# Cross-attention on one core: moving the last output pieces, two additions, and the closing matmuls of the last sequence

## Chip, cores and metric

The kernel runs on one core of a Trainium2 chip. Its time is device time in microseconds (us), the median of repeated runs. A profile is one further execution, taken by the hardware profiler. Engines are named as the profile names them: PE is the matmul engine (PEld its weight loads), DVE the vector engine, ACT the scalar engine, POOL the GpSimd engine, SP the engine that issues all DMAs of this kernel. L460 is line 460 of the kernel.

## What is computed

There are 32 sequences of 512 queries and 640 channels, each with its own context of 77 keys with 1024 channels, and 20 heads of 32 channels. The reference splits the keys into four sets, but the context has exactly the 77 keys of the first set, so the other three sets are empty and only this remains:

```
q = heads(x @ to_q_w)                       # (32, 20, 512, 32)
k = heads(ctx @ to_k_w); v = heads(ctx @ to_v_w)
s = einsum('bhqd,bhkd->bhqk', q, k) / sqrt(32)
p = softmax(s, axis=-1)
o = merge(einsum('bhqk,bhkd->bhqd', p, v))
out = o @ to_out_w + to_out_b + x
```

All of it is fp32. The kernel splits every fp32 operand of a matmul in a high and a low part and adds up three products, so most matmuls come in threes.

## The kernel before

Keys and values of all sequences are computed first and kept in DRAM. The rest of the program is a line of 160 **slots**, `slot(n)`, with n = 5b + j: sequence b (0 to 31) and a group j (0 to 4) of four heads. Below, "slot 159" is the last one, and P158 means the softmax numerators of slot 158. The instructions of each engine run in the order in which the Python code emits them (`tc.manual_schedule`); nothing is reordered later. An engine waits at an instruction until its inputs and its buffer are there, and all behind it on that engine waits too.

What happens to one slot's data:

- `scores(n, t)` (L354): three matmuls for each of four query tiles t of 128 rows into a PSUM tile `sc` (three buffers), and a maximum on DVE (L376).
- `exps(n, t)` (L382): four exponentials with row sums on ACT (L386), which free the `sc` buffer.
- `sums` and `normalize` (L394, L399), one slot later: reciprocal on DVE (L396) and one multiplication of the whole slot on POOL (L401).
- `transpose_p` (L405): a 32x32 block transposition on DVE (L408) into `z`, and four DMAs of 160 KB to a DRAM scratch tile `pd` (L415).
- `load_p` (L421): two DMAs from `pd` to the tile `raw` (L424, L425), now with keys on the partitions.
- `cast_p`, `rest_p`, `last_p` (L428 to L448): the split of `raw` in high and low parts `pp` (one buffer): ACT L432 and L438, DVE L439, POOL L446. DVE L439 needs ACT L432, POOL L446 needs ACT L438.
- `values(n)` (L454): eight matmuls into `pa`. The first needs L432, the second L439, the seventh L446.
- `split_a` (L468): the result `at`, in two parts, by ACT L104 and DVE L105. `take(n)` is `values` and `split_a`.

**Output.** A sequence's output is four row tiles t by two column halves h; each (t, h) is 15 matmuls (`project`, three for each of five groups j) into a PSUM bank `po` (three buffers). `piece(b, i)` emits twelve of these matmuls, the i-th of ten pieces; the pieces of sequence b are spread over the slots of the sequence after it. `finish()` adds each closed (t, h) to the residual tile `xr` on DVE (L518), which frees its bank, and after h = 1 sends the row tile out by one DMA of 320 KB (L522). `add_bias` (L483, POOL) adds the bias to a residual tile before that.

**Lag.** The values of a slot are taken three slots later: slot 159 takes P156. What is left then is in `end()`: the values of slots 157, 158 and 159, pieces 6 to 9 of sequence 30, and the whole output of sequence 31, which has only banks that have come free (`begin(i, j0, j1)` opens and adds groups j0 to j1 of its i-th (t, h); i = 7 takes the bank of `pa`).

**PE's order around the end, before.** Scores 0, 1, 2 of slot 159; piece 4 of sequence 30; values 156; scores 3; pieces 5, 6, 7, 8; values 157; piece 9 and `begin` for i = 0, 1 (24 matmuls in all); values 158; 60 matmuls of `begin`; values 159; `begin(6)`, `begin(7)`, and the 24 closing matmuls. A bank is reused every third (t, h): (2,1) of sequence 30 takes that of (1,0), (3,0) that of (1,1), and (3,1), which the last three matmuls of piece 8 open, that of (2,0).

**DVE's order there, before.** ... addition of (1,0); maximum 2; transposition of P158; maximum 3; addition of (1,1); L105 of 156; L439 of 157; reciprocal of 159; transposition of P159; additions of (2,0) and (2,1); L105 of 157; L439 of 158; additions of (3,0) and (3,1); ...

**SP's order there, before.** Four DMAs `pd` of P158; output (1); `raw` of 158; four DMAs `pd` of P159; output (2); `raw` of 159; residuals 0 and 1 of sequence 31; output (3); residuals 3 and 2; at the end the four outputs of sequence 31.

Of the kernel before, what the change touches and what calls it, by code (L numbers as in the profile page):

```python
# [23 lines left out]
P = 128  # L24
# [26 lines left out]
def kernel(  # L51
# [223 lines left out]
    def split_x(b, c, engine=nc.gpsimd):  # L275

        xt = main.tile([P, 2, S], FPR, tag="xt", name="xt", bufs=7)
        src = xss[b].rearrange("p (a t) u -> p t a u", t=NQ)[:, :, :, c * Q : (c + 1) * Q]
        parts = [xt[:, i, :].rearrange("p (t a j) -> p t a j", t=NQ, j=Q) for i in range(2)]
        nc.scalar.copy(parts[0], src)  # L280
        engine.tensor_tensor(parts[1], src, parts[0].bitcast(F32), ALU.subtract)  # L281
        xts[b, c] = xt
# [71 lines left out]
    def scores(n, t):  # L354
        b, j = divmod(n, NC_)
        g = GROUP_OF[j]
        qt, (kb, kc) = qts[n % 2], kbs[g]
        jg = j - GROUPS[g][0]
        sc = ps.tile([P, S], F32, tag="sc", name="sc", bufs=3)
        half = KCOLS // 2  # L360
        for m, (cols, keys_) in enumerate(
            (
                (slice(0, KCOLS), kb[:, jg]),
                (slice(0, half), kc[:, jg, 0]),
                (slice(half, KCOLS), kc[:, jg, 1]),
            )
        ):
            nc.tensor.matmul(  # L368
                sc[:, cols],
                qt[:, m, t * P : (t + 1) * P],  # L370
                keys_,
                start=(m == 0),
                stop=(m == 2),
            )
        nm = main.tile([P, HPC], F32, tag="nm", name="nm", bufs=3)
        nc.vector.tensor_reduce(  # L376
            nm, sc[:, :KCOLS].rearrange("p (h k) -> p h k", k=NKEY), AX.X, ALU.max, negate=True
        )
        return sc, nm

    def exps(n, t, sc, nm):
        if t == 0:  # L382
            sms[n] = main.tile([P, NQ * HPC], F32, tag="sm", name="sm", bufs=2)
        for i in range(HPC):
            at = t * HPC + i
            nc.scalar.activation(  # L386
                pnb[n % 2][:, at, :NKEY],
                sc[:, i * NKEY : (i + 1) * NKEY],
                AF.Exp,
                bias=nm[:, i : i + 1],  # L390
                accum_out=sms[n][:, at : at + 1],
            )
# [12 lines left out]
    def transpose_p(n):  # L405

        pn = pnb[n % 2]
        nc.vector.transpose(  # L408
            z.rearrange("p b t j -> p t b j"),
            pn.rearrange("p (t h) k -> p t (h k)", t=NQ).rearrange("p t (b i) -> p t b i", i=Q),  # L410
        )
        pd = dram.tile([NBLK * Q, S], F32, tag="pd", name="pd", bufs=6)
        rows = pd.rearrange("(b i) q -> i b q", i=Q)
        for a in range(4):
            nc.sync.dma_start(  # L415
                rows[:, :, a * P : (a + 1) * P],
                z[a * Q : (a + 1) * Q].rearrange("p b t j -> p b (t j)"),
            )
        pds[n] = pd
# [92 lines left out]
    def finish():  # L512

        while closed:
            b, t, h = closed.pop(0)
            xr = xrs[b, t]
            cols = slice(h * HALF, (h + 1) * HALF)
            nc.vector.tensor_tensor(  # L518
                xr[:, cols], pos.pop((b, t, h))[:, :HALF], xr[:, cols], ALU.add
            )  # L520
            if h == 1:
                nc.sync.dma_start(out[b, t * P : (t + 1) * P, :], xr)  # L522

    LATE = 4
# [15 lines left out]
    def take(m):  # L540
        values(m)
        split_a(m)
# [14 lines left out]
    def slot(n, beside=None):  # L557
        b, j = divmod(n, NC_)
        ahead, more = n + 1 < N, b + 1 < B
        back, first = PIECES[j]  # L560
        bo_, has_out = b - back, b >= back
        xsplits = SPLIT_X.get(j, ((), ())) if more else ((), ())
        turns = TRANSPOSE_X.get(j, ((), (), ())) if more else ((), (), ())
        taken, second = takes.get(n), seconds.get(n)

        refill(b, j, 0)
        if taken is not None:
            cast_p(taken)
        s = scores(n, 0)
        if taken is not None:  # L570
            rest_p(taken)
        if n:
            normalize(n - 1, sums(n - 1))
        if taken is not None:
            last_p(taken)
        exps(n, 0, *s)
        if ahead:
            queries(n + 1, 0, 2)
        s = scores(n, 1)
        if n - LAG + 1 in pds and n > LATE:  # L580
            load_p(n - LAG + 1)
        refill(b, j, 1)
        finish()
        if j == 4 and b + 2 < B:
            load_x(b + 2, (0, 1))
        if j in RESIDUAL and b >= RESIDUAL[j][0]:
            load_residual(b - RESIDUAL[j][0], RESIDUAL[j][1])
        if j in BIAS and b >= BIAS[j][0]:
            add_bias(b - BIAS[j][0], BIAS[j][1])
        exps(n, 1, *s)  # L590
        for i in turns[0]:
            transpose_x(b + 1, i)
        if ahead:
            queries(n + 1, 2, NC_)
        s = scores(n, 2)
        if n:
            transpose_p(n - 1)
        if ahead:
            split_q(n + 1)
        exps(n, 2, *s)  # L600
        if j == 4 and b + 2 < B:
            load_x(b + 2, (2, 3))
        for c in xsplits[0]:
            split_x(b + 1, c)
        if has_out:
            piece(bo_, first)
        if taken is not None:
            values(taken)
        if beside:
            beside()  # L610
        s = scores(n, 3)
        finish()
        for i in turns[1]:
            transpose_x(b + 1, i)
        if taken is not None:
            split_a(taken)
        for c in xsplits[1]:
            split_x(b + 1, c)
        exps(n, 3, *s)
        if has_out:  # L620
            piece(bo_, first + 1)
        for i in turns[2]:
            transpose_x(b + 1, i)
        if second is not None:
            cast_p(second)
            rest_p(second)
            last_p(second)
            take(second)
            if second + 2 in pds and second + 2 not in takes.values():
                load_p(second + 2)  # L630

    def end():


        last = B - 1
        load_p(N - 2)
        cast_p(N - 3)
        rest_p(N - 3)
        last_p(N - 3)
        normalize(N - 1, sums(N - 1))  # L640
        transpose_p(N - 1)
        finish()
        add_bias(last - 1, 3)
        piece(last - 1, 6)
        piece(last - 1, 7)
        finish()
        load_p(N - 1)
        load_residual(last, 0)
        load_residual(last, 1)
        piece(last - 1, 8)  # L650
        take(N - 3)
        piece(last - 1, 9)
        cast_p(N - 2)
        rest_p(N - 2)
        last_p(N - 2)
        finish()
        spare = late[0].tile([P, 3, S], F32, tag="raw", name="xr", bufs=2)
        load_residual(last, 3, spare.rearrange("p k q -> p (k q)")[:, :C])
        load_residual(last, 2)

        def begin(i, j0, j1):
            t, h = divmod(i, 2)
            if j0 == 0:
                if i < 3:
                    pos[last, t, h] = ps.tile([P, S], F32, tag="sc", name="po", bufs=3)
                elif i == 3:
                    pos[last, t, h] = ps.tile([P, S], F32, tag="pq", name="po", bufs=1)
                elif i < 7:
                    output_bank(last, t, h)
                else:  # L670
                    pos[last, t, h] = late[1].tile([P, S], F32, tag="pa", name="po", bufs=1)
            for j in range(j0, j1):
                project(last, t, h, j)

        begin(0, 0, 2)
        begin(1, 0, 2)
        take(N - 2)
        cast_p(N - 1)
        rest_p(N - 1)
        last_p(N - 1)  # L680
        for t in (0, 1, 3, 2):
            add_bias(last, t)
        begin(2, 0, 3)
        begin(0, 2, 4)
        begin(1, 2, 4)
        begin(2, 3, 4)
        for i in range(3, 6):
            begin(i, 0, 4)
        take(N - 1)
        begin(6, 0, 4)  # L690
        begin(7, 0, 4)
        for t in range(NQ):
            for h in range(2):
                project(last, t, h, 4)
                closed.append((last, t, h))
            finish()

    with tc.manual_schedule(engines=ENGINES):
        g0, gn = GROUPS_KV[-1]
# [72 lines left out]
```

## Time and profile before

| | us |
|---|---|
| median of 3 runs (2009.55 to 2010.04) | 2010.02 |
| profiled execution, its own time | 1996.0 |
| span of its instructions (all that the profile shows) | 1994.2 |
| PE busy / PEld busy | 1950.5 / 1760.0 |
| ACT busy / DVE busy / POOL busy | 1598.2 / 1352.5 / 982.8 |
| the last stretch, from scores 0 of slot 159 on (from 1946.86) | 47.3 |

Read it so: PE is the engine that is nearly always busy (98% of the span), with a granted clock of 0.991 of full speed on average, so time is gained or lost where PE stands still or runs at a lower clock. The table's last row is the span less 1946.86, the start of these matmuls in the timeline. All that the change touches lies there; before that the program is the same.

Durations that the timeline shows there, at full clock, and that are used below: three score matmuls 0.33, twelve `po` matmuls 1.80, eight `pa` matmuls 1.87, so 0.15 for a `po` matmul and 0.23 for a `pa` matmul.

### The profile page before, as it was taken

How to read it: one execution, taken by the hardware profiler on the slowest of the kernel's cores; microseconds unless marked ns; L12 is line 12 of the kernel's file. 1: busy time of each engine (PE TensorE's matmuls, PEld its weight loads, DVE VectorE, ACT ScalarE, POOL GpSimd, SP SyncE). 2: the span in 40 equal slices, each digit the busy share in tenths (PEclk: the TensorE clock that was granted, in tenths of full speed). 3: DMA queues.
4: the chain of work that ended last, by engine and by line, in shares of the span. 5: the costliest groups of instructions: out<-in, count | busy, mean ns of one | idle time of the engine just before them, and what ended most of it. 6: DMA issues, size and time to landing. Idle time of an engine off the chain costs nothing.

```text
span 1994.2 us, 38184 instructions
## 1 busy us (share of the span) xinstructions
PE 1950.5 (98%) x11012; PEld 1760.0 (88%) x11012; DVE 1352.5 (68%) x2159; ACT 1598.2 (80%) x6377; POOL 982.8 (49%) x617
## 2 busy tenths in 40 slices
PE   8999997899999999999999999999999999999998
PEld 7889986788899999899899898999989898988997
DVE  4443225777777777777777777777777777777774
ACT  3321128899999999999899999999999899998993
POOL 0000023555555555655556655566655566555554
PEclk9999998999999999999999999999999999999999
DMA  7994366889988889898988899998888888888975
GB/s 172 225 261 107 106 148 146 232 213 232 226 225 226 229 221 231 216 229 212 232 225 224 220 225 230 229 233 222 219 223 223 223 223 225 224 218 230 228 198 164
DMA packets 555997, 423.54 MB, mean 212 GB/s; under 512 B 170192, under 2 KB 459502, under 8 KB 555790
## 3 DMA queue, kind: packets, MB, share of 16 engines
q1 hardware_dynamic: 555789, 421.10, 83.9%
q8 instruction: 91, 1.49, 0.3%
q14 instruction: 117, 0.95, 0.2%
HBM read 245.61 MB, written 175.32 MB: 211 GB/s over the span
## 4 chain that ended last, share of the span: by engine, by line
PE 78%; DMA 9%; SPq 4%; POOL 3%; ACT 2%; issue 2%; DVE 2%; DVEq 0%; ACTq 0%; POOLq 0%
PE po L490 24%; PE pq L333 24%; PE pa L460 13%; PE sc L368 9%; PE pv L197 4%; PE pk L168 4%; DMA raw<-pd 3%; POOL pn L401 2%; DMA pd<-z 2%; SPq L114 1%; DMA xs<-in_x_dram 1%; POOL pp L446 1%; ACT pn L386 1%; DMA k_dram<-ks 1%; DMA cs<-in_ctx_dram 1%
## 5 line engine op out<-in xcount | busy, mean ns | idle before, releaser
L386 ACT ACTIVATE pn<-sc,nm 128x77 f32<-128x77 f32 x2560 | 802.0, 330 | 44.6 <-DVE nm L376 33.8
L401 POOL TENSOR_TENSOR pn<-pn,rs 128x1232 f32<-128x1232 f32 x160 | 364.4, 2277 | 670.3 <-DVE rs L396 643.9
L490 PE MATMUL po<-wo_s,at 128*128 128x320 f32 x3840 | 626.9, 312 | 2.2 <-DVE xr L518 2.2
L333 PE MATMUL pq<-xt,wq_s 128*128 128x512 f32 x2400 | 622.4, 400 | 0.0
L490 PEld LDWEIGHTS po<-wo_s,at 128*128 128x128 f32 x3840 | 566.3, 189 | 2.7 <-DVE xr L518 2.5
L386 ACT ACTIVATION_READ_ACCUMULATOR pn<-sc,nm 128x1 f32 x2560 | 533.1, 208 | 0.0
L333 PEld LDWEIGHTS pq<-xt,wq_s 128*128 128x128 f32 x2400 | 429.6, 190 | 77.4 <-POOL xt L281 0.2
L376 DVE TENSOR_REDUCE nm<-sc 128x4 f32<-128x308 f32 x640 | 294.6, 460 | 298.2 <-PE sc L368 291.0
L460 PE MATMUL pa<-pp,vb 128*128 128x512 f32 x1280 | 334.9, 402 | 18.4 <-ACT pp L432 9.8
L460 PEld LDWEIGHTS pa<-pp,vb 128*128 128x128 f32 x1280 | 243.5, 198 | 62.8 <-POOL pp L446 14.3
L408 DVE STREAM_TRANSPOSE z<-pn 128x1280 f32<-128x1280 f32 x160 | 241.5, 1509 | 36.2 <-POOL pn L401 31.6
L439 DVE TENSOR_TENSOR pp<-raw,pp 128x1024 fp32r<-128x1024 f32 x160 | 196.1, 1226 | 82.4 <-ACT pp L432 72.2
L368 PEld LDWEIGHTS sc<-kc,qt 128*128 128x128 f32 x1280 | 212.8, 189 | 27.2 <-ACT qt L348 4.2
L446 POOL TENSOR_TENSOR pp<-raw,pp 64x512 fp32r<-64x512 f32 x160 | 209.4, 1309 | 37.0 <-ACT pp L438 19.8
L368 PE MATMUL sc<-kc,qt 128*128 128x154 f32 x1280 | 222.9, 255 | 4.5 <-DVE qt L350 3.9
L350 DVE TENSOR_TENSOR qt<-pq,qt 64x512 fp32r<-64x512 f32 x320 | 214.3, 670 | 7.5 <-ACT qt L344 3.1
L281 POOL TENSOR_TENSOR xt<-xs,xt 128x512 fp32r<-128x512 f32 x157 | 200.0, 1296 | 19.4 <-ACT xt L280 12.5
L483 POOL TENSOR_TENSOR xr<-xr,bias 128x640 f32<-128x640 f32 x128 | 201.3, 1573 | 9.7
L348 ACT CAST qt<-qt 64x512 fp32r<-64x512 f32 x320 | 198.8, 621 | 8.9
L368 PE MATMUL sc<-kb,qt 128*128 128x308 f32 x640 | 196.1, 306 | 1.2 <-ACT qt L344 1.2
L432 ACT CAST pp<-raw 128x1024 fp32r<-128x1024 f32 x160 | 170.1, 1063 | 29.7 <-DMA raw<-pd 28.9
L104 ACT CAST at<-pa 128x512 fp32r<-128x512 f32 x160 | 94.9, 593 | 82.2 <-PE pa L460 81.1
(41 smaller groups left out, 1530.8 us busy)
## 6 DMA issues: line engine op xcount, KB each, us to landing
pd<-z SPq DMA_DIRECT2D x640, 160.0 KB, 3.6
raw<-pd SPq DMA_DIRECT2D x160, 512.0 KB, 4.3
xs<-in_x_dram SPq DMA_DIRECT2D x128, 320.0 KB, 7.0
xr<-in_x_dram SPq DMA_DIRECT2D x128, 320.0 KB, 3.8
out_dram<-xr SPq DMA_DIRECT2D x128, 320.0 KB, 3.2
raw<-pd SPq DMA_DIRECT2D x160, 128.0 KB, 4.4
v_dram<-vs SPq DMA_DIRECT2D x19, 640.0 KB, 4.0
k_dram<-ks SPq DMA_DIRECT2D x80, 128.0 KB, 2.4
```

Source lines behind the costliest of these rows:

```text
L281: engine.tensor_tensor(parts[1], src, parts[0].bitcast(F32), ALU.subtract)
L333: nc.tensor.matmul(pqs[n], wq_s[:, k, a, j * P : (j + 1) * P], xts[b, k][:, c, :], start=(k == 0 and m == 0), stop=(k == NC_ - 1 and m == 2),)
L350: nc.vector.tensor_tensor(qt[r, 1 + w, :], pq[r], qt[r, 0, :].bitcast(F32), ALU.subtract)
L368: nc.tensor.matmul(sc[:, cols], qt[:, m, t * P : (t + 1) * P], keys_, start=(m == 0), stop=(m == 2),)
L376: nc.vector.tensor_reduce(nm, sc[:, :KCOLS].rearrange("p (h k) -> p h k", k=NKEY), AX.X, ALU.max, negate=True)
L386: nc.scalar.activation(pnb[n % 2][:, at, :NKEY], sc[:, i * NKEY : (i + 1) * NKEY], AF.Exp, bias=nm[:, i : i + 1], accum_out=sms[n][:, at : ...
L401: nc.gpsimd.tensor_tensor(pf, pf, rs.unsqueeze(2).to_broadcast([P, NQ * HPC, NKEY]), ALU.mult)
L408: nc.vector.transpose(z.rearrange("p b t j -> p t b j"), pn.rearrange("p (t h) k -> p t (h k)", t=NQ).rearrange("p t (b i) -> p t b i", i=Q),)
L446: nc.gpsimd.tensor_tensor(pp[64:, 4, :], raw[:64, 2, :], pp[:64, 4, :].bitcast(F32), ALU.subtract)
L460: nc.tensor.matmul(pas[n], vb[:, t, :, a], pp[:, c, :], start=(m == 0), stop=(m == len(PASSES) - 1),)
L483: nc.gpsimd.tensor_tensor(xrs[b, t], xrs[b, t], bias, ALU.add)
L490: nc.tensor.matmul(pos[b, t, h][:, :HALF], ats[b * NC_ + j][:, a, t * P : (t + 1) * P], wos[0][:, j, c, h * HALF : (h + 1) * HALF], start= ...
```

## The change

Four edits, all of them in what is emitted from the middle of slot 159 on:

1. In slot 159 (`not ahead`), the exponentials of tile 2 and piece 4 are emitted, then scores 3, then transposition 158, exponentials 3, the additions, piece 5, and only then `take(156)`. Piece 4 and 5 stand around scores 3, and values 156 come last.
2. In `end()`, piece 6, the addition of (2,0), piece 7 and the addition of (2,1) are emitted ahead of the transposition of P159 and its DMAs.
3. The 24 closing matmuls of sequence 31 are cut in two: after `begin(6)` row tiles 0 and 1 are closed, after `begin(7)` row tiles 2 and 3.
4. The very last row tile goes out in two DMAs of 160 KB, one for each half, in place of one of 320 KB.

```diff
-            if h == 1:
+            if (b, t) == (B - 1, NQ - 1):
+                nc.sync.dma_start(out[b, t * P : (t + 1) * P, cols], xr[:, cols])
+            elif h == 1:
                 nc.sync.dma_start(out[b, t * P : (t + 1) * P, :], xr)
...
         s = scores(n, 2)
+        if not ahead:
+            exps(n, 2, *s)
+            piece(bo_, first)
+            s = scores(n, 3)
         if n:
             transpose_p(n - 1)
         if ahead:
             split_q(n + 1)
-        exps(n, 2, *s)
+            exps(n, 2, *s)
...
+        if not ahead:
+            exps(n, 3, *s)
+            finish()
+            piece(bo_, first + 1)
+            take(taken)
+            return
...
         normalize(N - 1, sums(N - 1))
-        transpose_p(N - 1)
-        finish()
         add_bias(last - 1, 3)
         piece(last - 1, 6)
+        finish()
         piece(last - 1, 7)
         finish()
+        transpose_p(N - 1)
         load_p(N - 1)
...
-        begin(6, 0, 4)
-        begin(7, 0, 4)
-        for t in range(NQ):
+
+        def close(t):
             for h in range(2):
                 project(last, t, h, 4)
                 closed.append((last, t, h))
             finish()
+
+        begin(6, 0, 4)
+        close(0)
+        close(1)
+        begin(7, 0, 4)
+        close(2)
+        close(3)
```

The order that results on PE: scores 0, 1, 2; piece 4; scores 3; piece 5; values 156; pieces 6, 7, 8; values 157; from there as before, up to the closing matmuls. On DVE: maximum 2, maximum 3, transposition of P158, addition of (1,1), L105 of 156, L439 of 157, reciprocal of 159, additions of (2,0) and (2,1), transposition of P159. On ACT the four exponentials of tile 3 stand ahead of L104 of 156. POOL's order is unchanged. On SP, output (2) stands ahead of the four DMAs `pd` of P159.

## The prediction

> **What bounds the kernel now.** I read the chain of waits first, from scores 0 of slot 159 on (1946.86), because nothing before that changes. PE is the chain there, except in two places. In these lines (start, length, what):
>
> ```profile
> 1951.97 1.27 POOL pp L446
> 1953.24 0.04 issue
> 1953.28 1.22 PE pa L460 x2
> 1954.50 0.61 PE sc L368 x3
> ...
> 1960.48 2.28 POOL pn L401
> 1962.76 0.02 issue
> 1962.78 1.51 DVE z L408
> 1964.29 0.39 DVE xr L518
> 1964.68 0.04 issue
> 1964.72 0.71 PE po L490 x3
> ```
>
> The reader is to see two waits of PE. In the first, the seventh matmul of values 156 waits for POOL's L446, which stands behind POOL's multiplication of P158. In the second, the last three matmuls of piece 8 need the bank of (2,0), whose addition (L518) stands on DVE behind the transposition of P159, which waits for POOL's L401. Both waits stand at the head of PE's queue, so all of PE's remaining work moves with them.
>
> Second, the windows view, cut at the ends of these waits (stretch, its length, busy time of PE, PEld, DVE, ACT, POOL, granted PE clock, DMA share, GB/s):
>
> ```profile
> 1951.27:1953.28 2.01, 0.01 (x1) 0.00 (x0) 1.36 (x1) 1.14 (x8) 1.88 (x2) 1.00 0.90 206
> 1953.28:1962.53 9.25, 9.25 (x50) 8.80 (x50) 3.02 (x6) 3.38 (x11) 5.38 (x3) 0.82 0.68 178
> 1962.53:1964.72 2.19, 0.01 (x1) 0.00 (x0) 1.94 (x3) 0.00 (x0) 1.72 (x2) 1.00 0.01 4
> ...
> 1953.35:1956.75 3.40, 3.40 (x12) 3.21 (x13) 1.55 (x4) 1.63 (x8) 1.52 (x1) 0.50 0.70 142
> ```
>
> PE stands for 2.01 and for 2.19 us. After the first wait its clock is 0.50 for 3.40 us; after the second it stays at 1.00.
>
> Third, the timeline and the landing times, for what would bind once PE is early: the load of slot 158's P, and when ACT takes it.
>
> ```profile
> 1958.88 0.38 SPq L424 DMA_DIRECT2D raw<-pd  x1
> ...
> DMA to landing us min/median/max: 4.1/4.1/4.1
> ...
> 1967.34 0.59 ACT L104 CAST at<-pa 128x512 fp32r<-128x512 f32 x1 [8.85 <-PE pa L460]
> 1967.83 1.05 ACT L432 CAST pp<-raw 128x1024 fp32r<-128x1024 f32 x1
> ```
>
> This load lands at 1958.88 + 4.1 = 1962.98, and is used 4.85 us later, since ACT and the single `pp` buffer wait for values 157. That 4.85 is the cover that the change uses up.
>
> **Edit 1, values 156 last.** New order from the end of piece 4 (1949.70): scores 3 needs the first `sc` buffer, which the exponentials of tile 0 free at 1949.79, so with a hand-off of 0.06 PE waits 0.15 that it did not wait before. Then 0.33 + 1.80 (piece 5) put values 156 at 1951.98; its seventh matmul comes up at 1951.98 + 6 x 0.23 = 1953.4, and L446 ends at 1951.97 + 1.27 = 1953.24. The first wait is gone: 2.01 us. POOL's L446 doesn't move, since its inputs (cast and reciprocal ahead of 1949.5) are untouched. DVE's maximum 3 (0.48) falls into the idle time ahead of the transposition of P158 (1.34 us in the timeline), so slot 158's P isn't delayed; without that cover it would cost the load below up to 0.48. ACT's four exponentials (1.3 us) end at about 1953.7, ahead of L104 of 156 at 1953.95.
>
> The low clock goes too: the stretch of 9.25 us holds 2 `pa`, 3 score and 45 `po` matmuls, at full clock 0.47 + 0.33 + 6.75 = 7.55, so it cost 1.70. From both sides: 0, if the timed runs never had it, to 1.70. I take 1.70, the row.
>
> The Trainium skill, "TensorE: Matmul & The Clock Gate", in its part on the HAM clock gate, says that the clock falls to half after an idle window of about 3.4 us, and that the window runs free of the kernel. The row differs: 2.01 us of idle sufficed here, and 2.19 us did not, though both lasted far less than 3.4. By the page alone the term would be 0 and the sum 1.70 less; that the window runs free would also make the term vary between runs.
>
> **Edit 2, additions ahead of the last transposition.** (2,0) is closed by the first three matmuls of piece 6. DVE's sequence now: L104/L105 of 156 end at 1955.3; L432 of 157 at 1955.6; L439 (1.23) at 1956.9; reciprocal 1957.05; addition of (2,0) 1957.5. PE reaches the matmuls that need its bank at 1953.85 + 1.80 + 1.80 + 1.35 = 1958.8. The second wait is gone: 2.19 us. The two additions cost the transposition nothing, since POOL's L401 is the later one: L438 of 157 ends at 1956.1, L446 (1.76, beside L439) at 1957.95, L401 (2.28) at 1960.3, and the additions are over by 1957.9. So P159 is transposed 2.4 us earlier than at 1962.78.
>
> On SP, output (2) now stands ahead of the four `pd` DMAs of P159, and behind `raw` of 158 (issued until 1959.78). It is issued by 1960.2, 1.7 us before P159 needs the queue (1961.9). Nothing queued behind waits for it.
>
> **What is late next.** PE would reach values 158 at 1949.70 + 14.87 (scores 0.33; pieces 5 to 9, 9.00; values 156 and 157, 3.74; twelve `begin` matmuls, 1.80) + 0.15 = 1964.72, not at 1970.67. The load lands at 1962.98; L432 runs 1963.03 to 1964.09, L439 1964.1 to 1965.35. The second matmul of values 158 comes up at 1964.95 and waits 0.44; L446, which the seventh needs at 1966.56, ends at 1963.03 + 3.46 = 1966.5 (the same distance as 1967.83 to 1971.29 now). So a new wait of 0.44. Bounds: 0 if the load lands half a microsecond earlier (the smallest landing in the trace is 3.3); 1.3 if output (2), 320 KB, is interleaved with it at the 389 GB/s that the load shows (0.84 more). Restart of PE after a wait costs 0.26 (0.71 for three `po` matmuls at 1964.72, not 0.45); one goes, one comes.
>
> Slot 159: transposition until 1961.9, `pd` and `raw` 5.42 later as now (1964.32 to 1969.74), landing 4.2 later at 1971.5, L446 done 3.46 later at 1975.0. PE reaches values 159 after 60 `po` matmuls (8.99), at 1976.05, and needs L446 only 1.4 later: a cover of 2.4. Were it gone, every microsecond would be one of time.
>
> **Edits 3 and 4, the end.** The closing matmuls only change places. `begin(7)` needs `pa` free 1.35 after values 159; `begin(6)` alone takes 1.80. The additions (0.44 each, eight in 3.50) follow PE at its pace now and later. POOL's four bias additions end 6.14 after L446, at 1981.2, ahead of row tile 2 at about 1983.7; at worst 0 to 0.3. The four outputs move 1.31 MB in 1989.15 to 1992.75, which is 364 GB/s. Later the last two row tiles, 0.66 MB, start moving at the same distance before the end, so 1.8 us of the same rate end about where they do now. I take a gain of 0.1; bounds +0.5 (nothing queued) and -0.3 (rows of 1280 bytes at the 313 GB/s to which the load falls in its last 0.4 us).
>
> **Sum**, on the span of 1994.2: 2.01 + 1.70 + 2.19 - 0.15 - 0.44 + 0.1 = 5.4 us. The profiled execution took 1996.0 (1.8 around the span), and the timed runs 2010.02, 14 more, which the trace does not show; I take off the same 5.4: 2004.6. From no change, a measurement of this kernel can tell about 0.2%, 4.0 us, so the line for faster is 2006.0.
>
> **Rivals.**
>
> A (0.50): the forecast, 2004.6; its own range 2003.2 to 2005.8.
>
> B (0.27): the timed runs did not have the low clock. For: it depends on how a wait lies against some window of the clock's control, since two waits of like length ended differently. Against: three runs within 0.5 us, where a term of 1.70 that comes and goes would spread them. Then 5.4 - 1.7 = 3.7: 2006.3.
>
> C (0.13): the wait moves to values 158 with its upper bound, 1.3 in place of 0.44, and in half of these cases half a clock window (0.85) behind it: 5.4 - 0.9 - 0.8 = 3.7 to 4.5, together with B's missing term down to 2.0; 2005.5 to 2008. For: the cover of 4.85 is used up to the last bit. Against: the window before the wait is busy, unlike 1949.93 to 1953.35 ahead of the low clock.
>
> D, the other side (0.07): the round trip of slot 158's P through DRAM becomes the bound. Elsewhere in the trace the four `pd` DMAs took up to 7.7 us to land and `raw` up to 8.3:
>
> ```profile
> DMA to landing us min/median/max: 2.2/3.6/7.7
> ...
> DMA to landing us min/median/max: 3.3/4.3/8.3
> ```
>
> Here they took 4.0 at most and 4.1, so 7.9 more is possible. The wait at values 158 would be 0.44 + 7.9 with 1.7 of low clock behind it: 5.4 - 9.6 = -4.2, 2014.2. It turns slower from 3.7 us of lateness on (5.4 - 1.7). Before, 4.85 of it was hidden. Against: the queue is emptier here than in the loop, where the long landings lie.
>
> The change not doing what it says (0.03): one of the two waits stays because of a buffer that I missed; 2007 to 2008.
>
> **Chances and range.** Faster by over 0.2%: 0.95 of A, a third of B and C: 0.62 with roundings; slower is D, 0.08; the rest, 0.30, within. The range takes A's low end with 0.4 for the measurement, and reaches over B into C: 2002.8 to 2007.6, which leaves out D and the tail of C.
>
> **What would show it.** In the profile after: no PE wait on POOL L446 before 1954 nor on DVE L518 near 1958; granted clock 1.00 throughout; values 158 starting at 1964.7 and waiting less than 1 us for DVE L439; values 159 at about 1976 without a wait; last addition on DVE near 1985.6, span 1988.8. Wrong would be: a clock of 0.50 after any wait, L432 of 158 later than 1963.5, or values 159 waiting.

## The result, and the profile after

| us | before | changed |
|---|---|---|
| median of 22 runs of each | 2007.61 (1994.61 to 2013.66) | 1997.92 (1991.43 to 2005.77) |
| profiled execution, its own time | 1996.0 | 2003.16 |
| span | 1994.2 | 2001.4 |
| scores 0 of slot 159 start at | 1946.86 | 1959.29 |
| from there to the end of the span | 47.3 | 42.1 |

The ratio of the times is 0.9958, 95% interval 0.9945 to 0.997: faster by 8.4 us, 6.0 to 11.0. The forecast was 2004.6 with a range of 2002.8 to 2007.6, so the time lies under the range. Among the runs of the kernel before that belong to the experiments, three took 2108.52, 6653.61 and 6653.7 us; no ratio or median here holds them.

The table holds the first lesson. The profiled execution of the changed kernel is 7 us *longer* than that of the kernel before, and still its last stretch is 5.2 us shorter. The two programs are the same up to scores 0 of slot 159, and reach them 12.4 us apart: the executions scatter by more than the change is worth, and only the last stretch can be compared between two traces.

The chain of waits of the changed kernel in that stretch (start, length, what):

```profile
1967.28 4.32 DMA pd<-z
...
1971.72 3.76 DMA raw<-pd
...
1975.58 1.06 ACT pp L432
1976.64 0.02 issue
1976.66 1.24 DVE pp L439
1977.90 0.04 issue
1977.94 1.92 PE pa L460 x7
1979.86 8.83 PE po L490 x60
1988.69 1.87 PE pa L460 x8
1990.56 4.07 PE po L490 x28
1994.63 1.76 issue
1996.39 1.76 DVE xr L518 x4
```

Neither POOL's L446 ahead of values 156 nor DVE's L518 ahead of piece 8 is in it. In their place stands the way of P158 through DRAM (`pd`, `raw`) and its split, L432 and L439: seven of the eight matmuls of values 158 wait for it. From there to the end PE runs without a gap; the last four additions follow its last closings. The "issue" ahead of them is how the chain is followed back, not a gap of PE, as the windows view of the same kernel shows (stretch, length, busy time of PE, PEld, DVE, ACT, POOL, clock, DMA share, GB/s):

```profile
1959.29:1976.90 17.61, 17.61 (x114) 16.72 (x113) 10.86 (x18) 10.66 (x42) 10.72 (x6) 1.00 0.75 207
1976.90:1978.00 1.10, 0.58 (x5) 0.24 (x3) 1.10 (x2) 0.25 (x1) 0.72 (x1) 1.00 0.98 237
1978.00:1998.00 20.00, 19.62 (x123) 18.71 (x123) 6.66 (x13) 2.74 (x4) 8.91 (x6) 1.00 0.49 155
```

PE is busy all of the first 17.61 us, stands for 0.52 us in the second row, and the clock is 1.00 in all three. The new wait in the timeline of PE (start, length, matmuls, idle time before and its releaser):

```profile
1977.03 0.40 PE L460 MATMUL pa<-pp,vb 128*128 128x512 f32 x1
1977.94 1.92 PE L460 MATMUL pa<-pp,vb 128*128 128x512 f32 x7 [0.52 <-DVE pp L439]
```

The first matmul, which needs only L432, starts on time; the second waits 0.52 us for L439. The forecast had 0.44.

### The profile page after: what moved, and what is told of

It reads as the page before. It is cut to its first block, busy times and chain, and to the rows that moved or that the text cites. A ratio compares the mean times of both kernels' runs of the same rounds, so it can differ in the third digit from the quotient of the medians.

```text
span 2001.4 us, 38185 instructions
## 1 busy us (share of the span) xinstructions
PE 1954.0 (98%) x11012; PEld 1761.3 (88%) x11012; DVE 1352.6 (68%) x2159; ACT 1590.7 (79%) x6377; POOL 981.6 (49%) x617
## 4 chain that ended last, share of the span: by engine, by line
PE 69%; DMA 14%; POOL 4%; SPq 4%; issue 3%; ACT 3%; DVE 2%; POOLq 0%; DVEq 0%; ACTq 0%
PE pq L333 21%; PE po L490 21%; PE pa L460 11%; PE sc L368 8%; DMA raw<-pd 6%; PE pv L197 4%; PE pk L168 4%; DMA pd<-z 3%; POOL pn L401 3%; POOL pp L446 1%; ACT pp L432 1%; DMA xs<-in_x_dram 1%; ACT pn L386 1%; SPq L415 1%; SPq L114 1%
## 5 line engine op out<-in xcount | busy, mean ns | idle before, releaser
L401 POOL TENSOR_TENSOR pn<-pn,rs 128x1232 f32<-128x1232 f32 x160 | 364.2, 2276 | 681.9 <-DVE rs L396 659.3
L408 DVE STREAM_TRANSPOSE z<-pn 128x1280 f32<-128x1280 f32 x160 | 241.5, 1509 | 42.1 <-POOL pn L401 33.7
L439 DVE TENSOR_TENSOR pp<-raw,pp 128x1024 fp32r<-128x1024 f32 x160 | 196.1, 1226 | 96.7 <-ACT pp L432 83.3
L446 POOL TENSOR_TENSOR pp<-raw,pp 64x512 fp32r<-64x512 f32 x160 | 209.0, 1306 | 33.9 <-ACT pp L438 16.6
L432 ACT CAST pp<-raw 128x1024 fp32r<-128x1024 f32 x160 | 169.9, 1062 | 46.1 <-DMA raw<-pd 46.0
L104 ACT CAST at<-pa 128x512 fp32r<-128x512 f32 x160 | 94.8, 592 | 71.5 <-PE pa L460 69.5
```

The lines of the kernel that those rows point to most:

```text
L401: nc.gpsimd.tensor_tensor(pf, pf, rs.unsqueeze(2).to_broadcast([P, NQ * HPC, NKEY]), ALU.mult)
L408: nc.vector.transpose(z.rearrange("p b t j -> p t b j"), pn.rearrange("p (t h) k -> p t (h k)", t=NQ).rearrange("p t (b i) -> p t b i", i=Q),)
L446: nc.gpsimd.tensor_tensor(pp[64:, 4, :], raw[:64, 2, :], pp[:64, 4, :].bitcast(F32), ALU.subtract)
```

## The experiments

All measures of the last stretch are from one trace each; the ratio is that of the times to those of the kernel before, with its 95% interval. "Waits" are PE's waits inside the stretch.

| kernel | slot 159 at | last stretch | waits | ratio of the times |
|---|---|---|---|---|
| before | 1946.86 | 47.34 | 2.0, 2.2 | |
| b1 (before again) | 1965.65 | 46.65 | 2.0, 1.4 | 1.0013 (0.9996 to 1.003) |
| b2 (before again) | 1965.94 | 49.26 | 2.0, 3.0 | 1.0002 (0.9982 to 1.0021) |
| edits 3 and 4 alone | 1954.74 | 46.56 | 2.0, 1.4 | 1.0002 (0.9984 to 1.002) |
| edit 1 alone | 1955.36 | 46.54 | 3.5 | 1.0004 (0.9987 to 1.0021) |
| edit 2 alone | 1957.29 | 43.41 | 2.0 | 0.9989 (0.9974 to 1.0004) |
| edits 1 and 2 | 1958.01 | 41.89 | 0.3 | 0.9978 (0.9957 to 0.9998) |
| changed | 1959.29 | 42.11 | 0.5 | 0.9958 (0.9945 to 0.997) |
| a1 (changed again) | 1957.33 | 42.17 | 0.6 | 0.9976 (0.9956 to 0.9995) |
| a2 (changed again) | 1965.41 | 42.09 | 0.6 | 0.9974 (0.9959 to 0.999) |
| x1 (more begun) | 1961.63 | 41.27 | none | 0.9961 (0.9944 to 0.9979) |
| x1b (the same) | 1962.90 | 41.30 | none | 0.9976 (0.9956 to 0.9997) |

The first question was where the difference between 5.2 us, which the end explains in the two first traces, and 8.4 comes from: from an end that is longer in other executions of the kernel before (T), or from outside the end (H). The texts below use these two letters, and R for something that makes the changed kernel quicker beside the end.

### The kernel before, twice more (b1, b2)

No edit.

> The kernel before, unchanged, for a second trace of it. T (the end explains all of the gain): its last stretch, from scores 0 of slot 159 to the end of the span, is longer here than the 47.3 us of the first trace, 49 to 52, because the clock falls after the second wait too or a wait is longer. H (the end is worth 5.4 us, and the rest of the difference in the medians lies in the unchanged part before slot 159): the stretch is 46.5 to 48 again, with waits of about 2.0 and 2.2 us, and the start of slot 159 lies several us off 1946.9.

> The kernel before, a third trace and a measure of scatter: ratio to itself within 0.2% of 1. Last stretch 46.5 to 47.4. The end of the second wait comes 10.6 to 11.5 us after the end of the first in every trace of it, with a low clock between them or not, because POOL's chain (L446, L401, then DVE L408, L518) sets it.

Measured: 46.65 and 49.26 us. The first agrees with H (though its second wait is 1.4 us, not 2.2), the second with T, and b2's own forecast of 46.5 to 47.4 is missed: the end of the kernel before isn't one number. In b1 the clock fell after the first wait, as in the first trace, but only behind scores 3: these come at their full pace, and 45 `po` matmuls then take 8.34 us, at a clock of 0.55 in the first 3.53 of them, where b2, below, needs 6.79.

```profile
1972.07 0.74 PE L460 MATMUL pa<-pp,vb 128*128 128x512 f32 x2 [2.01 <-POOL pp L446]
...
1972.97 8.34 PE L490 MATMUL po<-wo_s,at 128*128 128x320 f32 x45
1982.76 0.71 PE L490 MATMUL po<-wo_s,at 128*128 128x320 f32 x3 [1.44 <-DVE xr L518]
```

In b2's chain the second wait ends so:

```profile
1972.36 0.75 PE pa L460 x2
1973.11 0.34 PE sc L368 x3
...
1978.81 2.28 POOL pn L401
...
1981.11 1.51 DVE z L408
...
1983.05 1.17 PE po L490 x3
1984.22 3.41 PE pa L460 x8
1987.63 4.17 PE po L490 x24
```

The last three lines are the first matmuls after the second wait. They took 1.17, 3.41 and 4.17 us; in the first trace of the kernel before the same matmuls took 0.71, 1.87 and 3.52, which is 2.65 less in all. The windows view of b2 says why:

```profile
1972.36:1980.00 7.64, 7.64 (x50) 7.35 (x50) 3.02 (x6) 3.37 (x11) 4.54 (x3) 1.00 0.68 165
1980.00:1983.05 3.05, 0.06 (x1) 0.00 (x0) 1.94 (x3) 0.00 (x0) 2.57 (x2) 0.84 0.35 135
...
1983.50:1987.00 3.50, 3.50 (x10) 2.83 (x10) 0.00 (x0) 0.00 (x0) 0.00 (x0) 0.50 0.97 201
```

Here the first wait left the clock at 1.00, and the second was followed by 0.50. And with a full clock between the waits PE reached the second wait earlier and stood 2.99 us, not 2.19. The end of the second wait, counted from the end of the first, was 11.44 us in the first trace (1953.28 to 1964.72), and 10.69 both in b1 (1972.07 to 1982.76) with the low clock in between and in b2 (1972.36 to 1983.05) without it; this is the other forecast for b2, 10.6 to 11.5, and it holds. That time is set by the chain from scores 3 over POOL and DVE, not by PE. So a low clock *between* the waits costs little: 11.44 - 10.69 = 0.75 where it catches scores 3 and the two matmuls ahead of them (1.22 and 0.61 in the first trace, 0.75 and 0.34 in b2), else nothing. A low clock *behind* the second wait cost 2.65 in b2.

### Edit 1 alone

```diff
+        if not ahead:
+            exps(n, 2, *s)
+            piece(bo_, first)
+            s = scores(n, 3)
...
+            take(taken)
+            return
```

> Edit 1 alone (values 156 after scores 3 and piece 5). Both theories: the first wait (2.0 us) is gone, but PE then comes 3.7 us earlier to the bank of (2,0), whose addition still stands behind the transposition of P159; that moves only 2.4 us earlier, so the second wait grows from 2.2 to about 3.5 us. Last stretch 45 us (47.3 - 3.7 + 1.3), or 46.7 with a low clock after the longer wait. T: the time is 4 us or more under that of before. H: 1 to 2.5 us under it.

Measured: stretch 46.54, one wait of 3.5 us, ratio 1.0004 (0.9987 to 1.0021). Its chain:

```profile
1966.63 2.28 POOL pn L401
1968.91 0.02 issue
1968.93 1.51 DVE z L408
1970.44 0.39 DVE xr L518
1970.83 0.04 issue
1970.88 0.71 PE po L490 x3
1971.58 3.00 PE pa L460 x8
1974.59 3.94 PE po L490 x24
```

The first wait is gone, and the second has grown to 3.5 us, with a low clock behind it: the last three lines take 7.65 us, 1.55 more than in the first trace of the kernel before. So the expected 46.7 with a low clock is what the trace has, and less these 1.55 it would be 45.0 (an estimate), the other number that was expected. In the times, edit 1 alone gains nothing that can be told: H's 1 to 2.5 us isn't shown, nor excluded by an interval that reaches to 2.6 us faster; T's 4 us is outside it.

### Edit 2 alone

```diff
-        transpose_p(N - 1)
-        finish()
         add_bias(last - 1, 3)
         piece(last - 1, 6)
+        finish()
         piece(last - 1, 7)
         finish()
+        transpose_p(N - 1)
```

> Edit 2 alone (pieces 6 and 7 and their additions ahead of the last transposition). Both: the first wait and its low clock stay (3.7 us), the second wait (2.2 us, and 0.26 of restart) is gone, and no new wait at values 158, which PE reaches 5 us after its load has landed. Last stretch 44.9 us. T: the time is 4 us or more under that of before. H: 2.4 us under it.

Measured: stretch 43.41, the first wait of 2.0 us alone, no low clock after it in this trace, and no wait at values 158.

```profile
1963.71 0.74 PE L460 MATMUL pa<-pp,vb 128*128 128x512 f32 x2 [2.01 <-POOL pp L446]
...
1964.62 7.24 PE L490 MATMUL po<-wo_s,at 128*128 128x320 f32 x48
```

Ratio 0.9989 (0.9974 to 1.0004), 2.2 us faster with an interval that reaches from 5.2 to -0.8: H's 2.4 fits, and T's 4 isn't excluded. The 1.5 us under the expected 44.9 fit the low clock that this execution didn't have (1.70 in the first trace).

### Edits 3 and 4 alone, and edits 1 and 2 without them

```diff
+            if (b, t) == (B - 1, NQ - 1):
+                nc.sync.dma_start(out[b, t * P : (t + 1) * P, cols], xr[:, cols])
...
+        begin(6, 0, 4)
+        close(0)
+        close(1)
+        begin(7, 0, 4)
+        close(2)
+        close(3)
```

> Edits 3 and 4 alone (closing in two parts, last row tile in two DMAs). Both waits stay. Last stretch 47.2 us (gain 0.1, bounds +0.5 and -0.3), the time as before within 0.5 us. T: a stretch of 49 or more, for the reason it gives for b1.

> Edits 1 and 2 without 3 and 4. H: last stretch as in the changed kernel within 0.3 us (42.0 to 42.4), time 4 to 6 us under before. R: 8 or more under before, if the surplus doesn't hang on edits 3 and 4.

Measured: 46.56 with edits 3 and 4 against 46.65 in b1, which has the same two waits; and 41.89 without them against 42.1 with them, where the wait at values 158 was 0.2 to 0.3 us shorter. What edits 3 and 4 touch lies behind the start of values 159, and from there to the end of the span all twelve traces, with these edits and without, take 12.8 to 12.9 us: the two are worth nothing that can be told.

### The changed kernel, twice more (a1, a2)

No edit.

> The changed kernel once more, unchanged. H: its last stretch is 41.7 to 42.4 us again (42.1 in its first trace), against 46.6 to 47.3 in the three traces with both waits, so the end is worth 4.5 to 5.3 us; its mean time then lies 4 to 6 us under the mean of the kernel before on this chip, and the 8.4 of the first comparison was in part the scatter of the runs. R (something beside the end makes the changed kernel quicker by some 3.5 us more): the mean lies 8 us or more under that of before again.

> The changed kernel, a third trace and a second repeat of its time. H: last stretch 41.7 to 42.4; mean 4 to 6 us under the mean of before and b2 together. R (a surplus beside the end): 8 or more under it.

Measured: stretches of 42.17 and 42.09, and ratios of 0.9976 (0.9956 to 0.9995) and 0.9974 (0.9959 to 0.999), which is 4.8 and 5.2 us faster. H holds; R, 8 us or more, didn't come again, though the intervals (1.0 to 8.8 and 2.0 to 8.2 us) don't exclude it.

### More begun work ahead of values 158 (x1, x1b)

```diff
-        begin(0, 0, 2)
-        begin(1, 0, 2)
+        for i in range(4):
+            begin(i, 0, 2)
         take(N - 2)
...
-        begin(2, 0, 3)
-        begin(0, 2, 4)
-        begin(1, 2, 4)
-        begin(2, 3, 4)
-        for i in range(3, 6):
+        for j in (2, 3):
+            for i in range(4):
+                begin(i, j, j + 1)
+        for i in range(4, 6):
             begin(i, 0, 4)
```

> The changed kernel with twelve begun matmuls (1.8 us) moved from behind values 158 to ahead of them. The wait at values 158 (0.5 to 0.9 us in the first trace, with L439 as its releaser) is covered: last stretch 41.1 to 41.5 us, no PE wait in it. If the wait only moves to values 159 (L446 was ready 3 us ahead there), 42.1 again.

> The version with more begun matmuls ahead of values 158, once more: last stretch 41.1 to 41.5, and the mean 0.5 to 1.5 us under that of a2 (less than the scatter of the means can show); 5.5 to 6.5 under before.

Measured: stretches of 41.27 and 41.30, no wait of PE in them. The chain of x1 from values 157 on:

```profile
1974.13 1.87 PE pa L460 x8
1976.00 5.29 PE po L490 x36
1981.30 1.86 PE pa L460 x8
1983.16 7.06 PE po L490 x48
1990.22 1.87 PE pa L460 x8
```

Values 158 and 159 (the second and the third line of eight matmuls) follow the `po` matmuls without a gap. In the trace this version beats both others, by 0.8 us against the changed kernel: the wait of 0.5 and the restart behind it. In the times, 0.9961 (0.9944 to 0.9979) and 0.9976 (0.9956 to 0.9997), it is faster than before and can't be told from the changed kernel.

## Why the prediction was wrong, and where it was right

**The step that failed** is the last of the sum: "the timed runs 2010.02, 14 more, which the trace does not show; I take off the same 5.4", with "0.4 for the measurement" at the low end of the range, and "three runs within 0.5 us" taken for the scatter. There is no fixed difference of 14 us between a profiled and a timed run. Every run of the changed kernel stands about 1.8 above its own span (2003.16 and 2001.4, 1996.29 and 1994.5, and so on), and so does the kernel before in the later groups (2014.03 and 2012.3, 1999.16 and 1997.4). The profiled execution of the kernel before was a short one, and the three runs were longer ones of the same scatter; that they agreed within 0.5 us hid it. Over 22 runs the kernel before goes from 1994.61 to 2013.66, with a standard deviation of 4.2 us, and its median is 2007.61; in the three later groups of runs it was 2004.27, 2006.15 and 2005.64. So the base was 2.4 us too high by the first group. From 2007.61 the same 5.4 us gives 2002.2, still 4.3 above the measured 1997.92; from the later groups it gives 1998.9 to 2000.8, and the two repeats of the changed kernel had medians of 1999.53 and 2000.61. A base with its scatter of some 4 us should have widened the range at both ends. (The chances ahead of the range are also off in the second place: their own terms give 0.61 for faster, not 0.62, and D is 0.07 in one place and 0.08 in the other.)

**The size of the gain.** Forecast 5.4. In the last stretch the first pair of traces has 5.2, which is in part luck, since the stretch of before varies: the mean of the three traces of before is 47.75, that of the three of the changed kernel 42.12, so 5.6, and single pairs give 4.5 to 7.2. The times say 8.4 (6.0 to 11.0) in the first comparison and 4.8 and 5.2 in the two repeats. 5.4 lies just outside the first interval and inside the other two. The surplus of the first is open: it didn't come again, and no trace shows work or waits that would make it (slot 159 starts at 1959.5 in the mean of the three traces of before, at 1960.7 in that of the changed kernel). That it is scatter of the first groups of runs fits, as all three intervals hold 6.0 to 8.2 us, but isn't shown. Nor is a difference between chips excluded: a1 and a2 ran on two chips, each beside the kernel before on the same one, and which chip the first comparison had isn't on record.

**Edit 1, first wait gone, 2.01:** right. Its L446 wait is missing from all three traces of the changed kernel, and the price of 0.15 us ahead of scores 3 came out as 0.22 (scores 3 take 0.55 us in the chains of x1 and of edit 1, not 0.33).

**The low clock, 1.70:** right in the sum for the first trace, wrong as a separate term. It follows from the runs that removing both waits takes away the low clock *and* what it hid: 2.01 + 10.69 - 7.55 = 5.15 us if the clock never falls (7.55 is the work between the waits at full clock), up to 0.75 more if it falls ahead of scores 3, and 2.65 more where it falls after the second wait (b2's 49.26 against b1's 46.65).

**Rival B** (3.7 us of gain without the low clock) was therefore priced wrongly: without it PE only stands longer at the second wait, 3.0 in b2 and not 2.2. Its reason was right in one half: the clock's fall does change between executions. After the first wait of 2.0 us it fell in the first trace, in b1 and in the run of edits 3 and 4, and not in b2 and in that of edit 2. The Trainium skill, "TensorE: Matmul & The Clock Gate", in its part on the HAM clock gate, has the window of the clock's control free-running, and that agrees with the same wait ending both ways. Its rule that it takes an idle window of some 3.4 us differs from what was measured: 2.0 us sufficed three times in five.

**Edit 2, second wait gone, 2.19:** right, with a chain of causes that edit 1's run confirms. Edit 1 alone gains 0.1 us of the stretch against b1 and 0.8 against the first trace, edit 2 alone 3.2 against b1 (46.65 less 43.41), and both together 4.5 (46.65 less 42.12). The gap is the low clock behind edit 1's long wait. With 1.55 taken off there, and 2.65 off b2, the stretches are 46.6 for before (b2; b1 has 46.65, its low clock being hidden), 45.0, 43.4 and 42.1 (an estimate from one trace of each edit alone): 1.6 and 3.2 nearly add up to the 4.5, and what is over, 0.3, is less than the new wait at values 158.

**The new wait at values 158, 0.44:** right, 0.5 to 0.6 in three traces, with L439 as its releaser, as the forecast had it. Relative to the start of slot 159, values 158 came 17.74 us later (forecast 17.86), values 159 29.24 (29.19), the end of the span 42.11 (41.94). Values 159 did not wait.

**Rival C** (the wait at its upper bound with a low clock behind it) and **rival D** (the round trip through DRAM, late by several us) did not come. The round trip is what PE waits for at values 158, but it is late by 0.5 us only: the load landed 3.8 us after its issue, that of P159 4.0, and the clock stayed at 1.00. Output (2), now ahead of P159's DMAs on SP, made neither late.

**Edits 3 and 4, 0.1:** nothing that can be told, which fits 0.1.

## What to carry to other kernels

Read the scatter of the runs before setting a time on a change: three runs that agree within 0.5 us and a profile 14 us away are two samples of one scatter, not an offset, and a gain of 5 us is read from the same stretch of several traces rather than from their spans. Two waits in a row on one engine can be one chain: here, taking the first away alone left a second of 3.5 us (1.4 to 3.0 with both), and a low clock behind it took most of what was won; a low clock between them is for the most part hidden by the second. So price them together as the time from the start of the first to the end of the last, less the work between. And where a transfer had cover, look what is left of it after the gain, and put work that is ready in front of it: twelve matmuls moved took the new wait away in two traces, though the times can't tell the 0.8 us.

## What the hardware showed that was not expected

The clock fell to 0.50 after waits of PE of 2.0 us in some executions and not in others of the same program; after 3.0 and 3.5 us it fell in the one trace of each, and after 0.3 to 0.6, 1.4 and 2.2 us it didn't.

The same instructions up to slot 159 took from 1946.9 to 1965.9 us in twelve traces. Part of it is there at the first multiplication of L401 in the first slot (304.4 to 312.7 us), and the rest builds up on the way: b2 is behind the first trace of the kernel before by 4.9 us there, and at the same instruction by 7.9 forty slots later, 14.0 at slot 80 and 19.0 at slot 120. Which waits carry it was not followed further.
